# Correlation joins of a two-layer vision kernel regrouped: a part in a small PSUM bank, copies moved to other engines

## The chip, the cores and the metric

The kernel runs on one core of one Trainium2 chip. The metric is the device time of one execution in microseconds (us); the median of several executions is compared. The engines named below are TensorE (PE, matrix products into PSUM), VectorE (DVE), ScalarE (ACT), GpSimd (POOL) and SyncE (SP), which only issues DMAs here. Each engine works off its own queue in order and waits for semaphores at the head of it.

## The reference, cut to what matters

Two layers over x of shape (8, 768, 32, 32), float32. With N = 1024 pixels, 12 heads of 64:

```python
# layer 0
q, k, v = ...                                   # x_flat @ W_qkv.T, of gn(x)
scores = var_v @ swapaxes(var_k, -2, -1) * scale   # variances over a head's 64 channels
out = softmax(scores) @ v
x = x + (out @ W_proj.T + b_proj)
# layer 1, feature = gn(x)
feat_n = feature / max(norm, EPS)
corr = stack([sum(feat_pad[:, :, r:h+r, c:w+c] * feat_n, axis=1) for r, c in offsets()])  # 28 rows
x = x + einsum('bchw,oc->bohw', concatenate([feature, corr]), conv_w) + conv_b
```

So layer 1 is a 768 x 768 product over the channels and, added to it, a 768 x 28 product with 28 correlation rows. The 28-row part is what the change is about.

## The kernel before, in words

**Products.** Values, projection and convolution are computed by a seven-product scheme for 2 x 2 blocks (Strassen-like): a unit is one of the products (g, p) with g one of three channel groups and p in 1 to 7. A unit is 12 matrix instructions. Products accumulate in PSUM banks named x, y and z (`BANK`), two slots for x and two for y and z together (`Banks`). When a unit is done, VectorE takes its bank and adds it into the result (`Wide.take`, line 1064). Two "small" banks (`other`, pool `smp`, bufs=2, tag "sm") serve everything else: transposes, norms, grams, the denominators `den`. Two more (`two_banks`, pool `avp`) hold the attention's products or, after it, the projection's `own`.

**Images.** Image b's attention (`Pair`, `Attention`) runs interleaved with the convolution of image b-1 (`Conv`, called convolution b-1 below), then comes image b's projection (`project`), then the next image's values. Convolution b-1 adds into the tile `xn` of the image that has been used up. Convolution 7 comes last and alone.

**Correlations.** `Corr.gram` makes eight grams an image on PE (line 1151); `out` copies each from its small bank to a window on VectorE (line 1163) and stores it; `diagonals`, `scale`, `gather` and `product` turn them into the 28 rows `cs`, copied to the partitions 0, 32, 64 and 96 (`FOUR` = 32). So up to four 28-row matmuls can stand in four row groups of the array.

**Joins.** The 28-row part of an output block (i, half) is added to the bank of the unit that ends that block. `Conv.more` says of which output a unit is the last; such units are held open (`Wide.held`) and `Wide.join` (line 1057) adds the parts of all held units one after another, each in its row group, and lets VectorE take them. The sizes of the joins are in `Wide.joined` and again in `Conv.units` (which gives the planned time): four, four, then two and two for images 0 to 5, six of two for image 6 (the last of them after the projection, see below). Image 7 is different: its correlations come too late for that, so the 12 parts are made apart (`corr_units`, `corr`, line 1344), two at a time, in turn in the small and in the attention's banks, and VectorE adds them (`corr_taken`).

**Image 6's set-aside operands.** Units (0,2) and (1,2) of convolution 6 are kept for the moment after image 7's projection, while its norm is computed. `set_aside` copies their operands (three half rows of `f`, two of `acc`) before they are overwritten: five ACT copies of 128x512 into tiles of the exponentials' pool `ex`.

**Order.** The order of each engine's queue is written by a planner at build time. `Clock` counts planned time: emitting a unit passes its planned cost (`T_US` 2.58, `CORR_US` 1.2 for a join, `STEP_US` 1.73 for an attention step, `GRAM_US` 1.4), and `later.after(us, job)` emits a job when the planned time has come; `after_dve` counts from the planned end of VectorE's work (0.15 + 0.00104 us an element, `Vector`). `Attention.can_run` lets four steps go when `AHEAD` = 3 steps of exponentials are there and the last is planned to end within 1.0 us. At run time only the order and the semaphores count.

**The end of an image's attention.** After the last four steps `sum_up_last` (matmuls in line 887) puts two `den` tiles in small banks, four matmuls (eight instructions) in all, each halved by `HD`; VectorE inverts them in four pieces (`invert`), which frees one bank after two pieces and the other after four. The pair before (hp 4) is finished by `finish`: VectorE multiplies its output `v` by the inverses `rd`, which come by DMA (`den<-inv`, then `rd<-den`). `project` begins with `sums.first` (`t1o` on VectorE) and its units follow on PE.

**Start.** `keep_warm(WARM)` issues products of the identity while the first image loads.

Of the kernel before, what the change touches and what calls it, by code (L numbers as in the profile page):

```python
# [54 lines left out]
EXP, SUM, STEP_US = 1.07, 1.15, 1.73  # L55
KV_US, T_US, CORR_US = 1.93, 2.58, 1.2
GRAM_US = 1.4
WARM, BRIDGE = 31, (3, 7)

# [111 lines left out]
def two_layers(ctx, tc, x, wkv, wproj, bproj, wconv, wcorr, bconv, out):  # L173
# [855 lines left out]
    class Wide:  # L1029
        def __init__(self, kind, name, acc, bias, operand, finished, more=None):  # L1030
            self.kind, self.name, self.acc, self.bias = kind, name, acc, bias
            self.operand, self.finished, self.more, self.held = operand, finished, more, []
            self.joined, self.home = [], None

        def place(self, i, hf):
            return self.acc[:, i, hf * HF : (hf + 1) * HF]
# [1 line left out]
        def unit(self, g, p, between=None):  # L1038
            w = t_stream.take(self.kind, g, p)
            pairs = [(w[:, k, :], self.operand(p, k)) for k in range(JH)]  # L1040
            taken = lambda ps: self.take(g, p, ps)
            more = self.more(g, p) if self.more else None
            if more is None:
                banks.product(g, p, T_US, HF, pairs, taken, self.home if g == 2 else None)
            else:
                apart = (g, p) == (0, 2) and self.joined[:1] == [4]
                self.held.append((*banks.begin(g, p, HF, pairs, stop=False, between=between, apart=apart), taken, *more))
                if len(self.held) == (self.joined[0] if self.joined else 2):
                    self.joined = self.joined[1:]
                    self.join()  # L1050
            t_stream.fill()
# [67 lines left out]
    class Corr:  # L1119
# [18 lines left out]
        def gram(self, t):  # L1138

            b = self.b  # L1140
            tall = min(TALL, H - 4 * t)
            n = tall * WIDE
            if t not in self.turned:
                self.turn(t)
            block = self.turned[t]
            ps = other([P, SPAN], f"gr{b}_{t}")
            for j in range(J):
                image = self.f[:, j, :].rearrange("p (y x) -> p y x", x=W)
                for side in range(2):
                    left = side * (HW - 3)  # L1150
                    nc.tensor.matmul(  # L1151
                        ps[side * HD : (side + 1) * HD, :n].rearrange("p (y x) -> p y x", x=WIDE),
                        lhsT=block[:, j, side, :],
                        rhs=image[:, 4 * t : 4 * t + tall, left : left + WIDE],
                        start=j == 0, stop=j == J - 1,
                    )
            for ahead in range(t + 1, min(t + (3 if b == NB - 1 else 2), MT)):
                if ahead not in self.turned:
                    self.turn(ahead)

            def out():
                win = wins[t % 2 if t < MT - 1 else 2]
                vector.tensor_copy(win[:, :n], ps[:, :n])
                for side in range(2):
                    to = windowed[b % 2][t : t + 1, side * (HD * PITCH + HD - 3) :]
                    nc.sync.dma_start(
                        out=windows(to, (HW * PITCH - 3, 4), (PITCH, HW), (1, WIN)), in_=win[side * HD : (side + 1) * HD, :]
                    )
                if t % 4 == 3:
                    later.after(4.0, lambda: self.diagonals(t // 4))  # L1170

            later.after(GRAM_US + 0.25, out)
# [50 lines left out]
        def gather(self):  # L1223

            b, r = self.b, rows[self.b % 2]
            u = cs.rearrange("p a n -> p (a n)")[0:NCH, 0:N]
            v = uvpool.tile([NCH, N], F32, tag="uv", name=f"v{b}")
            nc.sync.dma_start(out=v[NS:NCH, :], in_=windows(r[0:1, PAD:], (0, NS + 4), (1, N)))
            nc.sync.dma_start(out=u[2 * NS : NCH, :], in_=windows(r[1:2, PAD:], (0, 4), (1, N)))
            for n, (first, apart) in enumerate(PICKED):  # L1230
                k, row = 3 * n, 2 + AHEAD_OF.index(first)
                nc.sync.dma_start(out=u[k : k + 3, :], in_=windows(r[row : row + 1, PAD:], (apart * ROW, 3), (1, N)))
                nc.sync.dma_start(out=v[k : k + 3, :], in_=windows(r[0:1, PAD + first :], (apart, 3), (1, N)))
                nc.sync.dma_start(
                    out=u[NS + k : NS + k + 3, :],
                    in_=windows(r[row : row + 1, PAD - first :], (apart * (ROW - 1), 3), (1, N)),
                )

            def product():
                vector.tensor_tensor(u, u, v, ALU.mult)  # L1240
                vector.tensor_tensor(cs[0:NCH, 2, :], cs[0:NCH, 0, :], cs[0:NCH, 1, :], ALU.subtract)
                for n in range(1, 4):
                    nc.sync.dma_start(out=cs[n * FOUR : n * FOUR + NCH, :, :], in_=cs[0:NCH, :, :])
                later.after_dve(6.0, lambda: ready.add(("cs", b)))

            later.after(18.0, product)

    class Conv:


        def __init__(self, b, f, acc, after):
            self.b, self.f, self.acc, self.after = b, f, acc, after
            self.early, self.then = False, None
            self.turn = False
            self.apart = [] if b < NB - 1 else [(i, hf) for i in (0, 3, 1, 4, 2, 5) for hf in range(2)]
            self.parts = {(i, hf, "f") for i in range(J) for hf in range(2)} | {(*q, "c") for q in self.apart}
            self.sums = TokenSums(f"f{b}", [f[:, k, :] for k in range(JH)], [f[:, JH + k, :] for k in range(JH)])

        def residual(self, n):
            nc.sync.dma_start(out=self.acc[:, n, :], in_=x1_dram[self.b][:, n, :])  # L1260
# [6 lines left out]
        def start(self):  # L1267
            if self.early:
                for n, us in ((3, 0.0), (4, 1.5), (5, 8.0)):
                    later.after(us, lambda n=n: self.residual(n))  # L1270
            if self.b == NB - 1:
                self.sums.third = [expool.tile([P, N], F32, tag="ex", name=f"t3_{k}")[:, :HF] for k in range(JH)]
            later.after(3.5, self.sums.second)
            self.wide = Wide(
                "c", f"c{self.b}", self.acc, bconv_sb, self.sums.operand, lambda i, hf: self.done(i, hf, "f"), self.more
            )
            self.wide.joined = [4, 4] if self.b < NB - 2 else []
            ready.add(("acc", self.b))
            later.after(7.0, self.thirds)

        def more(self, g, p):


            if p not in (2, 3, 7, 4) or self.apart:
                return None
            return g + JH * (p in (7, 4)), {2: 0, 3: 1, 7: 1, 4: 2}[p]

        def thirds(self):
# [6 lines left out]
            ready.add(("fourth", self.b))  # L1295

        def units(self):
            b, held, sizes = self.b, 0, [4, 4] if self.b < NB - 2 else []
            need = {7: (("third", b),), 4: (("fourth", b),)}
            out = []  # L1300
            for g, p in conv_order(b):
# [12 lines left out]

        def set_aside(self):

            first, second, third = [expool.tile([P, 2, HF], F32, tag="ex", name=f"held{n}") for n in range(3)]
            self.high = [first[:, 0, :], first[:, 1, :], second[:, 0, :]]
            self.low = {g: third[:, g, :] for g in range(2)}
            for k in range(JH):  # L1320
                act_copy(0.55, self.high[k], self.f[:, JH + k, :HF])
            for g in range(2):
                act_copy(0.55, self.low[g], self.acc[:, g, :HF])

            def operand(p, k):
                return self.high[k]
# [4 lines left out]

        def corr_units(self):
            return [
                (CORR_US, (("cs", self.b),), lambda n=n: self.corr(self.apart[n : n + 2])) for n in range(0, len(self.apart), 2)
            ]

        def corr(self, parts):

            self.turn = not self.turn
            av = None if self.turn else two_banks(f"av{self.b}_{parts[0][0]}")  # L1340
            for n, (i, hf) in enumerate(parts):
                at = slice(n * FOUR, n * FOUR + NCH)
                ps = other([P, HF], f"cc{self.b}_{i}_{hf}") if av is None else av[n]
                nc.tensor.matmul(ps, lhsT=wcorr_sb[at, i, :], rhs=cs[at, hf, :], start=True, stop=True)
                later.after(1.0, lambda i=i, hf=hf, ps=ps: self.corr_taken(i, hf, ps))

# [171 lines left out]
    for b in range(NB + 1):  # L1518
# [8 lines left out]
        if b:  # L1527
# [25 lines left out]
                    rest.insert(len(rest) - 3, (0.0, (), conv.set_aside))  # L1553
            else:
                units, parts = conv.units(), conv.corr_units()
                rest += [first, start] + units[:2] + grams + units[2:18]
                for n, unit in enumerate(units[18:]):
                    rest += parts[2 * n : 2 * n + 2] + [unit]
        else:
            more = [(us, (("xn", 1),) * (n > 1), unit) for n, (us, _, unit) in enumerate(kv1.units(0))]  # L1560
            rest.insert(len(rest) - 3, (0.0, (), lambda: apply_second(0)))
# [53 lines left out]
```

## Time and profile before

| | us |
|---|---|
| median of 3 executions | 2602.87 (2601.61 to 2604.66) |
| profiled execution, device time | 2601.92 |
| its span, first to last instruction | 2599.4 |
| L350 units and values on PE | 65% of the chain (34 + 17 + 9 + 5) |
| L800 attention on PE | 25% of the chain |
| L1057 joins, `y` and `z` shares of the chain | 1% each, rounded |
| L1344 parts of image 7 | 24 instructions, 7.5 us busy |

PE, PEld, DVE, ACT and POOL stand for the engines, PEld for TensorE's weight loads. "SPq" rows are DMAs as SyncE issues them; the time of such a row is that of issuing, not of landing. A timeline's row gives the start, the time, engine, line, operation, out<-in, shapes and a count; in brackets stands the idle time ahead of it and what ended that. In the chain the rows are the work that ended last, followed back. Most VectorE rows have the line of a helper, L167, and are told apart by tile names. A matmul here is two instructions (float32). Busy times of PE overlap, so the time of a group is read from the start of one group to the start of the next.

### The profile page before, as it was taken

Reading aid. Unit: us, or ns where it says so; the run is one execution under the profiler, and the core shown is the slowest. Engines: PE = TensorE matmul, PEld = TensorE weight load, DVE = VectorE, ACT = ScalarE, POOL = GpSimd, SP = SyncE. Lnnn points to the kernel's source line nnn. Section 1 sums busy time; section 2 is a strip of 40 time slices with the busy share of each in tenths; the row PEclk is TensorE's granted clock in tenths of the full one; section 3 lists DMA queues with packets and bytes.
Section 4 is the critical chain, followed back from the end, with each engine's and each line's share of the span. In section 5 each row is a group of like instructions: output and inputs, shape, how many; then the busy total and the mean of one; then the engine's idle time right before and its main releaser. Section 6 shows DMA issues by size and latency. Waiting matters only on the chain.

```text
span 2599.4 us, 40526 instructions
## 1 busy us (share of the span) xinstructions
PE 2586.6 (100%) x14776; PEld 1351.1 (52%) x14776; DVE 1609.8 (62%) x4118; ACT 1368.6 (53%) x1841; POOL 416.0 (16%) x444
## 2 busy tenths in 40 slices
PE   9999999999999999999999999999999999999999
PEld 5654465434664347643476435764356643575333
DVE  6868735775347853488535885357853578535764
ACT  1497179701797017970189701896018960199500
POOL 4320130004300043000330013300133001330000
PEclk9999999999999999999999999999999999999999
DMA  8866366355563655636556365463654636545323
GB/s 295 291 222 216 105 206 206 102 200 168 175 206 96 203 169 173 202 105 200 171 170 201 121 200 169 156 205 118 206 170 144 207 123 205 187 125 169 114 91 106
DMA packets 324716, 448.16 MB, mean 172 GB/s; under 512 B 59810, under 2 KB 245522, under 8 KB 324518
## 3 DMA queue, kind: packets, MB, share of 16 engines
q1 hardware_dynamic: 322454, 442.24, 53.0%
q10 hardware_dynamic: 2064, 3.34, 0.4%
q8 instruction: 117, 1.92, 0.3%
q14 instruction: 81, 0.66, 0.1%
HBM read 376.70 MB, written 64.40 MB: 170 GB/s over the span
## 4 chain that ended last, share of the span: by engine, by line
PE 96%; DVE 1%; DMA 1%; ACT 0%; issue 0%; POOL 0%; SPq 0%; DVEq 0%; ACTq 0%; POOLq 0%
PE x L350 34%; PE av L800 25%; PE y L350 17%; PE z L350 9%; PE own L350 5%; PE gr L1151 3%; PE den L831 1%; PE den L887 1%; PE y L1057 1%; PE z L1057 1%; ACT ex L774 0%; DMA bc<-vdr 0%; DVE acc L167 0%; DMA xn<-in_x_dram 0%; DVE bn L167 0%
## 5 line engine op out<-in xcount | busy, mean ns | idle before, releaser
L774 ACT ACTIVATE ex<-bc,nk 128x1024 f32<-128x1024 f32 x768 | 827.5, 1137 | 403.9 <-DMA bc<-vdr 206.1
L800 PE MATMUL av<-ex,v 128*64 128x512 f32 x3072 | 693.5, 593 | 1.2 <-ACT ex L774 1.1
L800 PEld LDWEIGHTS av<-ex,v 128*64 128x64 f32 x3072 | 332.2, 137 | 318.4 <-issue 199.3
L784 ACT ACTIVATE junk<-bk,vm 128x1024 bf16<-128x1024 f32 x368 | 420.4, 1142 | 28.8 <-DMA bk<-kdr 19.1
L167 DVE TENSOR_TENSOR acc<-acc,ex 128x1024 f32<-128x1024 f32 x300 | 345.2, 1211 | 0.8 <-ACT ex L774 0.8
L229 ACT COPY kp<-x 128x384 f32<-128x384 f32 x28 | 13.3, 478 | 524.1 <-PE x L350 515.4
L350 PE MATMUL y<-kv,s 128*64 128x384 f32 x1488 | 265.3, 487 | 0.3 <-POOL s L636 0.3
L350 PE MATMUL x<-kv,xn 128*64 128x384 f32 x1512 | 259.5, 486 | 0.0
L350 PE MATMUL x<-kv,s 128*64 128x384 f32 x1488 | 256.4, 486 | 0.0
L350 PEld LDWEIGHTS x<-kv,xn 128*64 128x64 f32 x1512 | 139.5, 137 | 104.0 <-issue 83.8
L350 PEld LDWEIGHTS x<-kv,s 128*64 128x64 f32 x1488 | 142.6, 137 | 93.3 <-issue 72.7
L350 PEld LDWEIGHTS y<-kv,s 128*64 128x64 f32 x1488 | 137.0, 137 | 89.9 <-issue 72.4
L530 POOL TENSOR_TENSOR rstda<-vea,neghalf 128x1 f32<-128x1 f32 x8 | 4.8, 595 | 958.6 <-DVE vea L167 958.6
L1136 POOL TENSOR_TENSOR turn<-f,ones 128x384 f32<-128x384 f32 x112 | 110.9, 1010 | 242.7 <-PE gr L1151 165.7
L350 PE MATMUL z<-kv,xn 128*64 128x384 f32 x768 | 133.7, 486 | 0.0
L350 PE MATMUL x<-f,wt 128*64 128x512 f32 x504 | 118.3, 592 | 0.0
L167 DVE TENSOR_TENSOR v<-y,v 128x128 f32<-128x128 f32 x180 | 40.9, 282 | 122.2 <-PE y L350 122.2
L636 POOL TENSOR_TENSOR s<-xn 128x384 f32<-128x384 f32 x64 | 65.6, 1035 | 304.3 <-PE x L350 190.0
L167 DVE BATCH_NORM_STATS2 vbn<-v 128x6 f32<-128x64 f32 x720 | 101.6, 209 | 0.0
L350 PEld LDWEIGHTS z<-kv,xn 128*64 128x64 f32 x768 | 74.9, 137 | 47.3 <-issue 36.6
L167 DVE SCALAR_TENSOR_TENSOR xn<-x,bconv_sb,xn 128x512 f32<-128x512 f32 x63 | 46.3, 745 | 80.8 <-PE x L350 79.7
L1151 PEld LDWEIGHTS gr<-f,turn 128*64 128x64 f32 x1344 | 87.8, 136 | 13.0 <-issue 4.8
(202 smaller groups left out, 3132.3 us busy)
## 6 DMA issues: line engine op xcount, KB each, us to landing
kv<-kvs SPq DMA_DIRECT2D x124, 576.0 KB
kv<-in_wkv_dram SPq DMA_DIRECT2D x95, 576.0 KB
bc<-vdr SPq DMA_DIRECT2D x96, 512.0 KB
f<-in_x_dram SPq DMA_DIRECT2D x48, 512.0 KB
bk<-kdr SPq DMA_DIRECT2D x46, 512.0 KB
x1d<-f SPq DMA_DIRECT2D x42, 512.0 KB
xn<-x1d SPq DMA_DIRECT2D x42, 512.0 KB
out_dram<-xn SPq DMA_DIRECT2D x82, 256.0 KB
```

The costliest lines, as they stand in the source:

```text
L167: return getattr(self.engine, name)(*args, **kw)
L229: nc.scalar.copy(to, at)
L350: nc.tensor.matmul(out[at], lhsT=lhsT[:, at], rhs=rhs, start=start, stop=stop, **kw)
L636: nc.gpsimd.tensor_tensor(self.sums[g][:, 0], a[g][2], a[g][3], ALU.add)
L774: nc.scalar.activation(ex, self.bc[e], AF.Exp, scale=self.kv.nk[self.half][:, h, t : t + 1])
L784: nc.scalar.activation(junk, self.bk[e], AF.Exp, scale=self.kv.m2[self.half][:, h, t : t + 1], accum_out=self.sums[:, e, t : t + 1],)
L800: nc.tensor.matmul(self.av[hf][e * HD : (e + 1) * HD, :], lhsT=self.vt[:, t, e, :], rhs=exs[e][:, hf * HF : (hf + 1) * HF], start=t == 0, ...
L831: nc.tensor.matmul(den[at * 32 : (at + 1) * 32, :], lhsT=ones[:, 0:32], rhs=self.acc[e][:, hf * HF : (hf + 1) * HF], start=True, stop=True,)
L887: nc.tensor.matmul(den[e * HD : (e + 1) * HD, :], lhsT=ones, rhs=self.acc[e][:, at], start=True, stop=True)
L1057: nc.tensor.matmul(t, lhsT=wcorr_sb[at, i, :], rhs=cs[at, tokens, :], start=False, stop=True, skip_group_check=True)
L1136: nc.gpsimd.tensor_tensor(to[:, :, side], half, windows(ones, ones.ap[0], (0, J), (HW, 4), (1, HW)), ALU.mult)
L1151: nc.tensor.matmul(ps[side * HD : (side + 1) * HD, :n].rearrange("p (y x) -> p y x", x=WIDE), lhsT=block[:, j, side, :], rhs=image[:, 4 * ...
```

## The change

Nothing that is computed changes. The parts:

- Images 0 to 5: joins of four, four and three, where the third join carries a fourth matmul in the free row group. It makes the part (5, 1), that of unit (2,7), in a small bank of its own (`Conv.single`); VectorE adds it with `corr_taken`, due 0.2 us after the join's own planned end. Unit (2,7) is no longer held, and unit (2,4) gets the first half's rows in place of the difference. Image 6: two, two, two, three with the extra one, and the two at the end as before.
- Image 7: its 12 parts in three groups of four, two in the small banks and two in the attention's; the first after unit 17 of the list instead of 18.
- Image 7's gram is copied by ACT, and the planner emits `product` 12 us after the gather instead of 18.
- `set_aside` uses three tiles of the pool `kv` and copies by a product with ones on POOL.
- `WARM` 31 becomes 42.

```diff
-WARM, BRIDGE = 31, (3, 7)
+WARM, BRIDGE = 42, (3, 7)
...
                 if len(self.held) == (self.joined[0] if self.joined else 2):
+                    if len(self.joined) == 1 and self.alone:
+                        later.after(T_US + CORR_US + 0.2, self.alone(len(self.held)))
                     self.joined = self.joined[1:]
                     self.join()
...
-                vector.tensor_copy(win[:, :n], ps[:, :n])
+                if b < NB - 1:
+                    vector.tensor_copy(win[:, :n], ps[:, :n])
+                else:
+                    act_copy(0.3, win[:, :n], ps[:, :n])
...
-            later.after(18.0, product)
+            later.after(18.0 if b < NB - 1 else 12.0, product)
...
+            self.alone = [(J - 1, 1)] if b < NB - 1 else []
+            self.parts = {(i, hf, "f") for i in range(J) for hf in range(2)} | {(*q, "c") for q in self.apart + self.alone}
...
+        def sizes(self):
+            return [4, 4, 3] if self.b < NB - 2 else [2, 2, 2, 3] if self.b == NB - 2 else []
+
+        def single(self, n):
+
+            i, hf = self.alone[0]
+            ps = other([P, HF], f"cc{self.b}_{i}_{hf}")
+            at = slice(n * FOUR, n * FOUR + NCH)
+            nc.tensor.matmul(ps, lhsT=wcorr_sb[at, i, :], rhs=cs[at, hf, :], start=True, stop=True)
+            return lambda: self.corr_taken(i, hf, ps)
...
-            self.wide.joined = [4, 4] if self.b < NB - 2 else []
+            self.wide.joined, self.wide.alone = self.sizes(), self.single
...
+            if g == JH - 1 and p in (7, 4):
+                return None if p == 7 else (J - 1, 0)
...
-            first, second, third = [expool.tile([P, 2, HF], F32, tag="ex", name=f"held{n}") for n in range(3)]
+            first, second, third = [
+                kvpool.tile([P, JH, KW], F32, tag="kv", name=f"held{n}")
+                .rearrange("p k m -> p (k m)")[:, :N].rearrange("p (n m) -> p n m", m=HF)
+                for n in range(3)
+            ]
+
+            def copy(to, at):
+                one = windows(ones, ones.ap[0], (0, HF // HD), (1, HD))
+                to, at = [a.rearrange("p (n d) -> p n d", d=HD) for a in (to, at)]
+                nc.gpsimd.tensor_tensor(to, at, one, ALU.mult)
...
-            self.turn = not self.turn
-            av = None if self.turn else two_banks(f"av{self.b}_{parts[0][0]}")
-            for n, (i, hf) in enumerate(parts):
+            some = [other([P, HF], f"cc{self.b}_{i}_{hf}") for i, hf in parts[:2]]
+            for n, (ps, (i, hf)) in enumerate(zip(some + two_banks(f"av{self.b}_{parts[0][0]}"), parts)):
                 at = slice(n * FOUR, n * FOUR + NCH)
-                ps = other([P, HF], f"cc{self.b}_{i}_{hf}") if av is None else av[n]
...
-                rest += [first, start] + units[:2] + grams + units[2:18]
-                for n, unit in enumerate(units[18:]):
-                    rest += parts[2 * n : 2 * n + 2] + [unit]
+                rest += [first, start] + units[:2] + grams + units[2:17]
+                for n, unit in enumerate(units[17:]):
+                    rest += parts[n : n + 1] + [unit]
```

More of the change, by code (lines that the diff above doesn't have):

```diff
@@ L1032, in __init__ @@
             self.operand, self.finished, self.more, self.held = operand, finished, more, []
-            self.joined, self.home = [], None
+            self.joined, self.home, self.alone = [], None, None
         def place(self, i, hf):
@@ L1253, in __init__ @@
             self.early, self.then = False, None
-            self.turn = False
             self.apart = [] if b < NB - 1 else [(i, hf) for i in (0, 3, 1, 4, 2, 5) for hf in range(2)]
-            self.parts = {(i, hf, "f") for i in range(J) for hf in range(2)} | {(*q, "c") for q in self.apart}
+            self.alone = [(J - 1, 1)] if b < NB - 1 else []
+            self.parts = {(i, hf, "f") for i in range(J) for hf in range(2)} | {(*q, "c") for q in self.apart + self.alone}
             self.sums = TokenSums(f"f{b}", [f[:, k, :] for k in range(JH)], [f[:, JH + k, :] for k in range(JH)])
+        def sizes(self):
[6 more added lines that the diff above has]
+            return lambda: self.corr_taken(i, hf, ps)
         def residual(self, n):
@@ L1297, in units @@
         def units(self):
-            b, held, sizes = self.b, 0, [4, 4] if self.b < NB - 2 else []
+            b, held, sizes = self.b, 0, self.sizes()
             need = {7: (("third", b),), 4: (("fourth", b),)}
@@ L1320, in set_aside @@
             for k in range(JH):
-                act_copy(0.55, self.high[k], self.f[:, JH + k, :HF])
+                copy(self.high[k], self.f[:, JH + k, :HF])
             for g in range(2):
-                act_copy(0.55, self.low[g], self.acc[:, g, :HF])
+                copy(self.low[g], self.acc[:, g, :HF])
             def operand(p, k):
@@ L1333, in corr_units @@
             return [
-                (CORR_US, (("cs", self.b),), lambda n=n: self.corr(self.apart[n : n + 2])) for n in range(0, len(self.apart), 2)
+                (CORR_US, (("cs", self.b),), lambda n=n: self.corr(self.apart[n : n + 4])) for n in range(0, len(self.apart), 4)
             ]
         def corr(self, parts):
-            self.turn = not self.turn
-            av = None if self.turn else two_banks(f"av{self.b}_{parts[0][0]}")
-            for n, (i, hf) in enumerate(parts):
+            some = [other([P, HF], f"cc{self.b}_{i}_{hf}") for i, hf in parts[:2]]
+            for n, (ps, (i, hf)) in enumerate(zip(some + two_banks(f"av{self.b}_{parts[0][0]}"), parts)):
                 at = slice(n * FOUR, n * FOUR + NCH)
-                ps = other([P, HF], f"cc{self.b}_{i}_{hf}") if av is None else av[n]
                 nc.tensor.matmul(ps, lhsT=wcorr_sb[at, i, :], rhs=cs[at, hf, :], start=True, stop=True)
```

## The prediction

> **What bounds the kernel now.** I read the page's busy shares and its chain first, then the waits of TensorE (engine, line, releaser: us in total, times, longest), then the stretch in which an image's convolution ends, in the chain and in the timelines of VectorE and SyncE.
>
> ```profile
> PE 2586.6 (100%) x14776; PEld 1351.1 (52%) x14776; DVE 1609.8 (62%) x4118; ACT 1368.6 (53%) x1841; POOL 416.0 (16%) x444
> ...
> PE 96%; DVE 1%; DMA 1%; ACT 0%; issue 0%; POOL 0%; SPq 0%; DVEq 0%; ACTq 0%; POOLq 0%
> ```
>
> ```profile
> PE gr L1151 <- DVE win L167: 2.0, 4, 1.0
> ...
> PE av L800 <- ACT ex L774: 1.1, 3, 0.6
> ```
>
> TensorE has work all the time, and its recorded waits come to under 9 us. So whatever leaves its queue is gained one to one, and whatever makes it wait is lost one to one; a wait of some us would be something this kernel hardly has anywhere. The end of convolution 1 (it recurs in 2 to 5 at the same distances), in the chain (start, us, what):
>
> ```profile
> 844.66 0.62 PE y L1057
> 845.29 0.01 PE x L1057
> 845.29 0.42 PE y L1057
> 845.72 0.01 PE x L1057
> 845.72 7.02 PE av L800 x32
> 852.74 2.58 PE z L350 x12
> 855.31 2.58 PE x L350 x12
> 857.89 0.62 PE z L1057
> ...
> 858.95 1.87 PE den L887 x8
> ```
>
> A join of two takes 844.66 to 845.72, 1.06 us. Right behind the last join come the two `den` products of `sum_up_last`, which take **both** small banks, and then the projection. The same stretch on VectorE and on SyncE's queue:
>
> ```profile
> 858.73 1.23 DVE L167 TENSOR_TENSOR v<-v,rd 128x1024 f32<-128x1024 f32 x1 [4.86 <-DMA rd<-den]
> 860.03 1.76 DVE L167 RECIPROCAL acc<-den 128x256 f32<-128x256 f32 x1
> 861.71 1.82 DVE L167 TENSOR_TENSOR t1o<-v 128x512 f32<-128x512 f32 x3
> 863.45 0.68 DVE L167 TENSOR_TENSOR xn<-z,xn 128x512 f32<-128x512 f32 x1
> ```
>
> ```profile
> 844.71 0.56 SPq L337 DMA_DIRECT2D wt<-tsp  x1
> 845.36 0.56 SPq L863 DMA_DIRECT2D den<-inv  x1
> 846.49 0.94 SPq L1356 DMA_DIRECT2D out_dram<-xn  x2
> 847.48 1.41 SPq L1540 DMA_DIRECT2D f<-in_x_dram  x3
> 848.99 1.20 SPq L876 DMA_DIRECT2D rd<-den  x2
> ```
>
> VectorE stands still for 4.86 us until the inverses `rd` land at 858.73; the convolution's results (`xn<-z`) are taken only at 863.45. Today nobody on TensorE waits for that.
>
> **What the change saves.** (1) Images 0 to 6 have one join less each. A join of four costs 476.10 to 477.17 in the chain, 1.07, no more than two; so the lone matmul in the fourth row group adds nothing to its join and 7 x 1.06 = 7.4 us go. (2) The last image: six pairs cost 2.42 + 1.92 + 1.92 = 6.3 in the chain (2581.09 to 2583.51, then twice 1.06 + 0.86); three fours at 1.07 cost 3.2. Each four is taken in 4 x 0.65 us beside a unit of 2.58 and its own take of 0.7, 3.3 of 3.64, so I give back 0.3 for banks taken late: 2.8. Its input must come earlier by one unit. Before, the product runs at 2576.64, its copies are issued by 2581.16 and the first use is at 2581.02. Six us earlier it stands behind the take at 2568.25 (0.69), with the gather's last issue at 2565.91; the copies then wait for weights until 2571.2 and are out by 2573.8, 4 us ahead of need. Free under that cover; each us beyond it would cost one. (3) The last image's gram copies on ACT: the waits shown come to 2.0 us. ACT is idle there but for 0.93 of turning per gram; a copy costs between VectorE's 0.30 and ACT's 0.48 for 384 columns, within a gram's 1.44. What stays is the store of each window, about 2.2 us of landing before its buffer is used again. Between 0 and 2.0 I take 1.2. (4) `set_aside`: its five ACT copies sit among the exponentials from 2440.86, two of them waiting 4.85. From 2445.44, 32 attention products and one unit last to the join at 2457.40, 11.96 us; in convolution 1 the same two pieces cost 6.92 + 2.68. So 2.3 us come back. On POOL the five cost 5 x 1.35 = 6.7 (an estimate, 384 columns take 1010 ns in L1136); nothing else stands in POOL's queue until 2518, the source is overwritten from 2458 and the copy read at 2514. If that cover went, the load of `f` would wait. The weights' buffers are free by then, as the last `kv` load is over. (5) More warm-up: 62 instructions end at 10.61, the last at 112 ns each, 22 more end near 13.1, before `mva` at 13.31. Between 0 and the 0.2 us by which the first units trail: 0.1. Sum of the savings: 7.4 + 2.8 + 1.2 + 2.3 + 0.1 = **13.8 us**.
>
> **What it adds: a wait for a small bank.** The lone matmul puts its part into one of the two small banks, and only `corr_taken` on VectorE frees it. Follow the planner's order in image 2, counted from the start of unit (2,7). That unit now passes 2.58, not 3.78. The last attention run may start if the last exponential, planned to end at 3.92, ends within 1.0 of now; 2.58 fails by 0.34, so unit (2,2) goes first and the run starts at 5.16 (either order leads to the same 12.08). At 12.08 unit (2,4) issues the lone matmul and the join. The eight additions of 1.215 from 5.16 end at 14.88, so `sum_up_last` comes at 15.38, inside (2,4)'s 3.78. `corr_taken` is due at 12.08 + 3.98 = 16.06. So the second `den` product stands in TensorE's queue ahead of the projection and must wait for an instruction that VectorE gets **behind** `v<-v,rd` (15.81), `t1o` (15.86) and three takes (15.96). The reciprocals that free the other bank come later still (16.58). Image 7's order is the same to within 0.2; in image 1 the `den` pair comes before (2,7) and the first of its banks is free, at 532.98, before the lone matmul, so convolution 0 only gains.
>
> Price, in convolution 1: without the first join, (2,4) ends at 856.7, the join at 857.8, the first `den` half (4 of 8, 0.86) at 858.6. VectorE: `rd` must land. The weight load of (2,2) now goes ahead of `den<-inv` on SyncE and holds it until that unit ends at 847.2, 2.5 later than today; the two stores (0.94 of issue, 0.5 MB) leave the queue ahead of `rd`. Both ends: 1.5 earlier or 1.5 later than 858.7; I take 859.2. Then 1.23 + 1.82 + 3 x 0.66 + 0.65 = 5.7 more: the bank is free at 864.8, the wait is **6.2 us** (4.2 to 7.7). Five times that is 31.0. In convolution 6, `rd` lands near 2457 and TensorE, freed of (4), is there at 2455.7: 6.9. Together 37.9. Behind the waiting matmul stands the whole projection; nothing fills the gap.
>
> A wait this long may also cool the clock. In the trace warm-up matmuls follow each other at 213 ns from 1.63 to 5.42 and at 112 ns afterwards, 1.8 us lost, although PEclk reads 1.00; a gap of 2.83 (10.6 to 13.45) left them at 112. So between 0 and 1.8 per wait; as 6.2 is farther from 2.83 than from nothing I have seen, I take 1.1, 6.6 for six. [...]
>
> **Sum.** 37.9 + 6.6 - 13.8 = +30.7 us. The profiled execution took 2601.92 (span 2599.4, 2.5 around it), so 2632.6; the median shown, 2602.87, lies 0.95 above it: **2633 us**, +1.2%.
>
> **Rivals.**
> *No wait: the bank is free in time* (11%). If `corr_taken` stands before the `den` pair, or the pair finds other space, only the savings are left: 2602.9 - 13.8 = 2589. For it: the added part was given a due time of its own. Against it: 15.38 against 16.06 by the kernel's own constants. This is the faster side.
> *A short wait* (5%). If VectorE takes the results while it waits for `rd` anyway, from 857.8 on, 1.98 + 0.65 frees the bank at 860.4: 1.8 us x 6 = 10.8, less 13.8: 2600. For it: the 4.86 of idleness. Against it: `v<-v,rd` is planned 0.25 ahead, and an engine's queue keeps its order.
> *The last image waits for its correlations instead* (2%). If the product comes too early for the gather, VectorE's takes stop; at one unit and both ends late, 5 us on top of the savings, 2594.
>
> **How the numbers follow.** The wait has 82%. Its own ends: six waits at 4.2 with no cooling, 25 - 14 = +11; six at 7.7 and 1.8 with savings of 11, 57 - 11 = +46. So **2611 to 2649**; that range alone holds nearly all of its 82%, and I keep 2610 to 2649 as the range, with the faster cases left outside. About 0.2% (5 us) is what a measurement of this kernel tells from no change. Faster: the first rival, the third and little of the second, 14%. Same: most of the second, 4%. Slower: 82%.
>
> **What would show it.** Right: in convolutions 1 to 6 a TensorE wait of 4 to 8 us at `den` L887, released by VectorE's `xn<-cc`, and nothing like it in convolution 0; joins at three an image; `gr <- win` waits below 1 us; ACT without `held`; after a wait, units longer than 2.58 if the clock cools. Wrong: `den` directly behind the join in all images, which gives about 2589; or the wait there but ended by an early take, about 2600.

## The result, and the profile after

The changed kernel takes 2630.24 us (median, 2628.27 to 2630.7) against 2602.87: a ratio of 1.0103, 95% interval 1.0088 to 1.0118. The profiled execution has a span of 2628.4 against 2599.4. The forecast was 2633, slower, by a wait for a small bank.

The page's busy shares and the shares of the chain by engine, after:

```profile
PE 2590.9 (99%) x14798; PEld 1350.4 (51%) x14798; DVE 1617.9 (62%) x4117; ACT 1367.7 (52%) x1844; POOL 426.7 (16%) x449
...
PE 95%; DMA 3%; DVE 2%; issue 0%; SPq 0%; POOL 0%; ACT 0%; ACTq 0%; DVEq 0%; POOLq 0%
```

Here one sees only that something other than TensorE is on the chain for a few per cent now. TensorE's waits (us in total, times, longest) name it:

```profile
PE den L887 <- DVE xn L167: 28.8, 6, 5.0
...
PE gr L1153 <- ACT win L229: 0.4, 2, 0.2
```

One new wait of any size, six times, in `den` (4.4 to 5.0 us each); the old waits for ACT's exponentials and for VectorE's gram copies are gone, and 0.4 us for ACT's gram copies is left. The end of convolution 1 again, first on TensorE, then on VectorE, then SyncE's queue:

```profile
856.53 0.69 PE L1272 MATMUL cc<-cs,wcorr_sb 28*128 28x512 f32 x1
...
857.60 1.08 PE L887 MATMUL den<-acc,ones 128*64 128x512 f32 x4
863.56 1.98 PE L887 MATMUL den<-acc,ones 128*64 128x512 f32 x4 [4.88 <-DVE xn L167]
865.33 4.15 PE L350 MATMUL x<-v,wt 128*64 128x512 f32 x12
869.31 2.74 PE L350 MATMUL own<-v,wt 128*64 128x512 f32 x12
```

```profile
858.03 1.23 DVE L167 TENSOR_TENSOR v<-v,rd 128x1024 f32<-128x1024 f32 x1 [3.52 <-DMA rd<-den]
859.17 1.89 DVE L167 TENSOR_TENSOR t1o<-v 128x512 f32<-128x512 f32 x3
860.97 0.68 DVE L167 TENSOR_TENSOR xn<-y,xn 128x512 f32<-128x512 f32 x1
...
862.83 0.68 DVE L167 TENSOR_TENSOR xn<-cc,xn 128x512 f32<-128x512 f32 x1
```

```profile
844.62 3.10 SPq L337 DMA_DIRECT2D wt<-tsp  x2
847.82 0.56 SPq L863 DMA_DIRECT2D den<-inv  x1
848.43 1.37 SPq L1566 DMA_DIRECT2D f<-in_x_dram  x3
850.22 1.12 SPq L876 DMA_DIRECT2D rd<-den  x2
```

The lone part `cc` is written from 856.53 on and read (`xn<-cc`) at 862.83. VectorE, idle since 854.51, waits for `rd` until 858.03, then does `v<-v,rd`, `t1o` and three takes. Only then the second half of `den` gets the bank. The second weight load goes ahead of `den<-inv`, as foreseen, which is issued at 847.82 instead of 845.36; `rd` still lands 0.7 us earlier here than before (858.03 against 858.73).

The row at 863.56 shows the other half of the loss: 1.98 us for four instructions that took 1.08 at 857.60, and 4.15 for a unit of 2.74. The windows (stretch, its length, busy us of PE, PEld, DVE, ACT and POOL, then the granted clock, the DMA share and GB/s) say why:

```profile
858.40:863.40 5.00, 0.28 (x2) 0.00 (x0) 5.00 (x8) 0.00 (x0) 0.00 (x0) 0.79 0.41 138
863.60:868.10 4.50, 4.50 (x12) 1.42 (x14) 1.57 (x1) 0.00 (x0) 0.00 (x0) 0.50 0.00 0
868.20:878.20 10.00, 10.00 (x48) 3.23 (x46) 6.06 (x8) 0.00 (x0) 0.00 (x0) 1.00 0.67 210
```

In the wait the clock is lowered to 0.50, and the first 4.5 us of work after it run at that. So it is in all six waits; in each of these stretches the clock is at 0.50 from end to end:

```profile
861.40:868.10 6.70, 4.54 (x12) 1.46 (x14) 3.77 (x5) 0.00 (x0) 0.00 (x0) 0.50 0.00 0
1189.10:1192.30 3.20, 2.81 (x8) 0.97 (x10) 2.00 (x2) 0.00 (x0) 0.00 (x0) 0.50 0.00 0
1513.40:1520.00 6.60, 4.93 (x12) 1.48 (x14) 3.28 (x4) 0.00 (x0) 0.00 (x0) 0.50 0.00 0
1841.00:1847.70 6.70, 5.87 (x14) 1.71 (x16) 2.44 (x3) 0.00 (x0) 0.00 (x0) 0.50 0.01 2
2168.70:2172.00 3.30, 3.02 (x8) 1.00 (x10) 1.89 (x2) 0.00 (x0) 0.00 (x0) 0.50 0.00 0
2489.60:2496.20 6.60, 5.78 (x14) 1.72 (x16) 2.43 (x3) 0.00 (x0) 0.00 (x0) 0.50 0.01 2
```

**A ledger.** From the first `own` matmul of one projection to that of the next, in us, from the traces; the columns E1 to E5 are the experiments below. The step of convolution 1 ends in the wait shown above.

| convolution | before | after | E1 | E3 | E4 | E5 |
|---|---|---|---|---|---|---|
| 1 | 320.25 | 326.42 | 319.05 | 321.13 | 324.61 | 320.25 |
| 2 | 320.25 | 325.10 | 319.05 | 320.69 | 324.04 | 320.25 |
| 3 | 320.25 | 326.63 | 319.05 | 320.96 | 324.82 | 320.25 |
| 4 | 320.24 | 327.21 | 319.05 | 320.73 | 325.11 | 320.25 |
| 5 | 320.25 | 325.72 | 319.05 | 320.83 | 324.91 | 320.25 |
| 6 | 318.59 | 322.84 | 314.98 | 315.87 | 319.79 | 316.17 |

### The profile page after: what moved, and what is told of

Its sections match the earlier page's. It is cut to its first block, busy times and chain, and to the rows that moved or that the text cites. A ratio compares the mean times of both kernels' runs of the same rounds, so it can differ in the third digit from the quotient of the medians.

```text
span 2628.4 us, 40564 instructions
## 1 busy us (share of the span) xinstructions
PE 2590.9 (99%) x14798; PEld 1350.4 (51%) x14798; DVE 1617.9 (62%) x4117; ACT 1367.7 (52%) x1844; POOL 426.7 (16%) x449
## 3 DMA queue, kind: packets, MB, share of 16 engines
q8 instruction: 118, 1.93, 0.3%
## 4 chain that ended last, share of the span: by engine, by line
PE 95%; DMA 3%; DVE 2%; issue 0%; SPq 0%; POOL 0%; ACT 0%; ACTq 0%; DVEq 0%; POOLq 0%
PE x L350 34%; PE av L800 23%; PE y L350 17%; PE z L350 9%; PE own L350 5%; PE gr L1153 3%; DMA rd<-den 2%; PE den L831 1%; PE den L887 1%; DVE xn L167 1%; DMA den<-inv 1%; DVE t1o L167 0%; DMA xn<-in_x_dram 0%; PE z L1059 0%; PE y L1059 0%
## 5 line engine op out<-in xcount | busy, mean ns | idle before, releaser
L350 PE MATMUL x<-v,wt 128*64 128x512 f32 x384 | 96.9, 640 | 0.0
```

Of the source, the lines that this page charges most:

```text
L350: nc.tensor.matmul(out[at], lhsT=lhsT[:, at], rhs=rhs, start=start, stop=stop, **kw)
```

## The experiments

**E1: the added part is taken first.** One due time is changed, so that `corr_taken` comes ahead of the `den` pair and of `v<-v,rd` on VectorE. In the planner's count of the prediction, where the `den` pair is written at 15.38, `v<-v,rd` at 15.81 and `t1o` at 15.86, `corr_taken` moves from 16.06 to 15.08; in E2 it comes at 15.68, in E3 at 15.84.

```diff
-                        later.after(T_US + CORR_US + 0.2, self.alone(len(self.held)))
+                        later.after(3.0, self.alone(len(self.held)))
```

> The changed kernel with corr_taken due 3.0 us after the join instead of 3.98, so that it stands ahead of the den pair and of v<-v,rd on VectorE; all else as changed. My theory (TensorE waits for a small bank that VectorE frees only behind rd, t1o and three takes, and cools in that time): the six waits of 4.4 to 5.0 us at L887 are gone, the clock stays full, and 28.8 us of waits and some 13.7 us of cold pace come off the changed kernel's 2630: about 2588, 0.6% below the kernel before. Rival (the den pair is slow for another reason, such as its additions or the inverses rd): the waits stay and the time stays near 2630.

Measured: 2586.08 us, 0.9933 of the kernel before (0.9920 to 0.9945). No wait at L887, clock 1.0 all through. On TensorE and VectorE at the same place:

```profile
857.66 1.94 PE L887 MATMUL den<-acc,ones 128*64 128x512 f32 x8
859.43 2.74 PE L350 MATMUL x<-v,wt 128*64 128x512 f32 x12
```

```profile
857.75 0.69 DVE L167 TENSOR_TENSOR xn<-cc,xn 128x512 f32<-128x512 f32 x1 [3.19 <-PE x L1059]
858.73 1.23 DVE L167 TENSOR_TENSOR v<-v,rd 128x1024 f32<-128x1024 f32 x1 [0.28 <-DMA rd<-den]
```

The take now uses time in which VectorE had nothing to do. So the whole loss hangs on the place of one 0.69 us instruction, once in each image, in a queue; the rival's cause is out. Summed over the six rows, after less E1 is 43.7 us.

**E2: after the den pair, but ahead of `v<-v,rd`.** As E1 with `later.after(3.6, ...)`.

> The same with 3.6 us: corr_taken now comes after the den pair in the order written, but still ahead of v<-v,rd on VectorE. Theory: what counts is VectorE's queue ahead of corr_taken, not which of the two was written first, so the time is that of the 3.0 us variant, about 2588, with no wait at L887. Rival (the bank must be handed over before the den pair is written, else TensorE stalls): near 2630.

Measured: 2585.14 us, 0.9930 (0.9914 to 0.9945), no wait at L887. That `den` is written before the instruction that frees its bank costs nothing; what stands ahead of that instruction on VectorE does.

**E3: directly behind `v<-v,rd`.** As E1 with `later.after(3.76, ...)`.

> The same with 3.76 us: corr_taken directly behind v<-v,rd, but ahead of t1o and the three takes. Theory: rd lands near 858.0 in convolution 1, v<-v,rd ends at 859.3, corr_taken at 859.9; the den half is ready at 858.5. So six waits of 1.3 to 1.6 us, too short to cool the clock (2.83 us at the start did not): 8 to 10 us over the 3.0 us variant, about 2597. Rival (t1o and the takes cost nothing, since rd is all that is waited for): waits of 4 us and more, above 2610.

Measured: 2595.98 us, 0.9973 (0.9962 to 0.9984), 9.9 over E1. TensorE's waits, then the place in convolution 1 on TensorE and VectorE:

```profile
PE den L887 <- DVE xn L167: 8.6, 6, 1.9
```

```profile
860.87 1.08 PE L887 MATMUL den<-acc,ones 128*64 128x512 f32 x4 [1.86 <-DVE xn L167]
```

```profile
858.99 1.23 DVE L167 TENSOR_TENSOR v<-v,rd 128x1024 f32<-128x1024 f32 x1 [4.15 <-DMA rd<-den]
860.13 0.68 DVE L167 TENSOR_TENSOR xn<-cc,xn 128x512 f32<-128x512 f32 x1
```

`rd` landed 0.96 later here (858.99 against 858.03; the `den` pair itself starts 0.33 later), and this is the longest of the six waits. With `t1o` and the takes behind it instead of ahead, the wait is short, and the clock stays at 1.0 in the record. The wait is thus made of two parts: `rd` with its product, and `t1o` and the takes.

**E4: the wait filled.** The changed kernel with products that nobody reads between the two halves, in images 2 to 7.

```diff
                 dens.append(den)
+                if hf and self.b > 1:
+                    fill = two_banks(f"fill{self.b}")[0]
+                    for n in range(20):
+                        nc.tensor.matmul(fill[:, 0:P], lhsT=ident, rhs=ident, start=True, stop=True)
```

> The changed kernel as it is, with 20 products of the identity (40 instructions of 112 ns, 4.5 us) put between the two den halves of images 2 to 7, into one of the attention's banks. Theory: the wait is filled, the clock is never lowered, and the cold pace (61% of a 27 us total, some 13.7 us) is saved although TensorE gets more work: about 2616. Rival (the lowered clock costs nothing, the whole loss is the waits): no change, 2630; if the products stand in the way, more than that.

(The 61% in it is a slip: it is half of 27 us of work at the lowered clock.) Measured: 2617.68 us, 1.0054 (1.0040 to 1.0068), 12.6 less than the changed kernel without the added work. On TensorE:

```profile
858.26 4.73 PE L894 MATMUL fill<-ident 128*128 128x128 f32 x40
863.67 1.08 PE L887 MATMUL den<-acc,ones 128*64 128x512 f32 x4 [0.68 <-DVE xn L167]
864.58 2.75 PE L350 MATMUL x<-v,wt 128*64 128x512 f32 x12
```

The bank comes no earlier, at 863.67, but the half takes 1.08 again and the unit 2.75. So the lowered clock is a loss of its own, beside the wait. Of the profiled executions E4's is 11.0 shorter (2628.4 less 2617.4) and not the whole 13.7 worked out below: over the six images the second halves start 2.9 us later after the first ones than in the changed kernel, most of it because `rd` landed later.

**E5: no lone part.** The changed kernel with the joins of before.

```diff
-            self.alone = [(J - 1, 1)] if b < NB - 1 else []
+            self.alone = []
...
-            return [4, 4, 3] if self.b < NB - 2 else [2, 2, 2, 3] if self.b == NB - 2 else []
+            return [4, 4] if self.b < NB - 2 else []
...
-            if g == JH - 1 and p in (7, 4):
-                return None if p == 7 else (J - 1, 0)
```

> The changed kernel with the lone part taken out again: joins of four, four, two and two (images 0 to 5) and of two (image 6) as before; all else as changed. Theory: no part stands in a small bank, so there is no wait at L887 and a full clock without moving any due time; seven joins of 1.06 us come back, so the time is that of the 3.0 us variant, 2586, plus 7.4: about 2593.5, still 0.35% below the kernel before. Rival (the loss belongs to another part of the change, the POOL copies or the image 7 order): above 2603.

Measured: 2595.03 us, 0.9970 (0.9960 to 0.9981). Convolutions 1 to 5 take the 320.25 of before to the hundredth; E1 saves 1.20 in each. Convolution 6 goes from 318.59 to 316.17 with its joins unchanged: 2.42 from `set_aside`. The other parts of the change are sound, then; the lone part alone made it slower.

**E6: image 7's parts in twos, from unit 18 on,** otherwise E1.

```diff
-                (CORR_US, (("cs", self.b),), lambda n=n: self.corr(self.apart[n : n + 4])) for n in range(0, len(self.apart), 4)
+                (CORR_US, (("cs", self.b),), lambda n=n: self.corr(self.apart[n : n + 2])) for n in range(0, len(self.apart), 2)
```

(`corr` and the list of units as before the change.)

> The 3.0 us variant with image 7's parts two at a time from unit 18 on, as before. Theory: three times 1.06 us more on TensorE, less some 0.2 of waiting between the fours: 2586 + 2.9 = about 2589. Rival (the end is bound by the takes on VectorE or by the stores, not by TensorE): no difference, 2586.

Measured: 2588.48 us, 0.9946 (0.9934 to 0.9959), 2.4 over E1, though the two intervals overlap. The traces are clearer: from the first gram of image 7 to the start of the last matmul 66.37 us against 63.85 in E1, 2.5 more. Most of the three added groups of 1.06 us, 2.5 of 3.2, shows up in the time, so here TensorE bounds the end.

**E7: image 7's gram copied by VectorE,** otherwise E1 (the `if b < NB - 1` of the change taken out).

> The 3.0 us variant with image 7's grams copied by VectorE again. Theory: the waits gr <- win come back, 2.0 instead of 0.4 us: 1.2 to 1.6 us more, about 2587.5, which a measurement can hardly tell from 2586; the waits of the profile show it. Rival (the windows' stores bound this stretch, whoever copies): waits stay below 1 us.

Measured: 2587.47 us, 0.9942 (0.9930 to 0.9955); by the medians not to be told from E1. The profile tells it: the waits are back,

```profile
PE gr L1153 <- DVE win L167: 2.0, 4, 1.0
```

and from the first gram to the last matmul it takes 65.83 us against 63.85, 2.0 more.

**E8: `set_aside` on ACT again,** into tiles of `ex`, otherwise E1.

> The 3.0 us variant with set_aside as before: five ACT copies into tiles of ex. Theory: attention's last steps of image 7 wait for ACT again, 2.3 to 2.5 us between their start and the join: about 2588.5. Rival (that stretch was slow for another reason, the order of the units): no difference, 2586.

Measured: 2591.34 us, 0.9958 (0.9944 to 0.9971), 5.3 over E1: the direction held, the size did not. Its own waits are only

```profile
PE av L800 <- ACT ex L774: 2.6, 2, 1.9
```

and the step to the next projection is 1.93 longer than E1's. Another 3.2 us lie in the projection behind it: with ACT's planned time longer, the planner wrote the last attention run after the join instead of before it, so the `den` products come three units later and a unit waits for `t2o`. Of the 3.2, 1.76 are the `den` products themselves, which now lie behind the mark that ends the step; 1.5 is what the two units that start with the wait for `t2o` take longer than in E1. So this run did not change one cost alone; the clean price of the copies is the 2.42 of E5.

## Why the prediction was right, point by point

- **The wait, its place and its cause:** shown. The planner's constants gave `den` before `corr_taken` and `v<-v,rd` before that; E1, E2 and E3 move the one instruction through these places and get no wait, no wait, and a short one.
- **Not in convolution 0, and in six others:** as the row of TensorE's waits says; the first of the six is the one at 863.56.
- **The size of the wait:** too large. I put `rd` at 859.2; it landed at 858.03. Whether the two stores that left SyncE's queue did that is not shown: with the same queue it landed at 858.73 in E1, as late as before. The rest of the way, 5.7 in the prediction, took 5.4 (858.03 to 863.43). The waits were 4.4 to 5.0 and not 6.2; six of them some 30 us (43.7 less the 13.7 of the next point; 28.8 as the profile counts idleness), not 37.9.
- **The clock:** too small: I took 1.1 as a middle of 0 and 1.8. It was lowered in all six waits. After each wait 2.9 to 6.0 us of work were left at 0.50, 27.5 us in all, of which half is lost at half the clock: 13.7, 2.3 a wait, and not 6.6. The upper end was too low because the start's 3.79 us of warm-up matmuls at 213 ns each were taken for the longest stretch at a slow pace (the granted clock reads 1.00 there, so that the pace and the lowered clock are one thing was my estimate). E4 shows this term by itself.
- **These two errors nearly cancel:** 43.7 measured against 44.5 predicted. The mechanism was right, but that the total came so close is luck: the total is better than its terms.
- **The savings:** 14.7 (2599.4 less E1's 2584.7) against 13.8. The joins gave 1.20 and not 1.06 each in convolutions 1 to 6 (convolution 0's does not stand out from the spread of that stretch); `set_aside` 2.4 against 2.3; grams 2.0 against 1.2, 1.6 of it in the waits shown, which fell from 2.0 to 0.4 where I had left 0.8; image 7's parts 2.5 against 2.8. In the profiles the additional warm-up can't be told apart: the first unit starts at 16.42 after and at 16.49 before, and between 16.1 and 17.2 in the experiments, as the image lands.
- **The savings by the medians** are larger, 17.0 (2603.1 for the kernel before, measured beside E1, less 2586.08). Of the kernel before, 15 of the 22 executions measured beside the experiments have a mean granted clock of 0.999 and not 1.0; beside E1 to E4 these took 2603.1 to 2605.3 and the others 2600.3 to 2601.6, beside E5 to E8 the two groups overlap. Of E1 to E8 one execution in 41 has 0.999. They all have the longer warm-up, which closes the gap of 2.83 at the start to 0.70 in the profile after, so it may be worth more than the 0.1 of the prediction. That is not shown: no execution of the kernel before at 0.999 was profiled.
- **Slips in the sum:** 2632.6 and 0.95 make 2633.6, and the lower end, +11, is 2614 and not 2611. Neither bears on the outcome.
- **The rival "no wait"** described E1: 2589 foretold, 2586 measured. The short wait by takes ahead of `rd` did not occur; the correlations of the last image were in time.

E1 and E2 beat both kernels: 0.7% below the kernel before.

## What to carry to other kernels

The small bank handed to a second user was free here when its reader had run, 0.68 us of work, and the reader ran when all that stood ahead of it in VectorE's queue had run: 5.4 us from the landing of `rd` to the free bank. Price that whole stretch, waits for DMAs included, before a small shared bank gets one more tenant. If the bound engine waits a few us, count the slow clock after the wait too: here waits of 4.4 to 5.0 us cost 28.8 and the slow clock another 13.7, almost half again, while E3's of up to 1.9 had no slow clock behind them. And ask where the freeing instruction could stand instead: six times 0.69 us moved into idle time was worth 44 us.

## What the runs showed of the hardware

- In the clock record of the changed kernel's trace the granted clock of 0.50 comes in six pieces, four of 6.827 us and two of 3.413, one to a wait, and the starts of these pieces lie whole multiples of 3.4133 apart (861.33 to 1189.01, 327.68, is 96 of them, 1189.01 to 1513.28, 324.27, is 95), though the waits themselves began 326.42 and 325.10 apart. Each began 2.65 to 4.59 us after the end of TensorE's last instruction before the wait. So waits of almost the same length cost differently here: the one of 4.94 us left 3.07 us of slow work (1.5 lost), the one of 5.00 us left 5.96 (3.0 lost). What sets these lengths and places is not shown.
- E3's waits of up to 1.9 us did not lower it, and the waits of up to 1.2 us that E4's added work left did not either: the granted clock is 1.0 over both profiled executions. The gap of 2.83 us at the start of the kernel before did not slow the matmuls in the profiled execution: warm-up matmuls follow each other at 112 ns behind it (13.87 to 14.32) as ahead of it.
- A join carries a fourth 28-row matmul in another row group for nothing (856.53 to 857.60, 1.07 us, against 1.06 for a join of two), and one join less in an image saves 1.20 us where its own row reads 1.06.
